# Start-up loads of a fused convolution, Fourier and feed-forward kernel: Fourier matrices issued after the other weights, small loads issued by ScalarE

## The chip, the cores and the metric

The kernel runs on one core of a Trainium2 chip. The time is the device time of one launch in microseconds (us); lower is better. One core has a matrix engine (TensorE, PE in the profile), three engines for elementwise work (VectorE or DVE, ScalarE or ACT, GpSimd or POOL) and SyncE (SP), which in this kernel issues nearly all DMA transfers. Each engine executes its own instruction stream in order; engines wait for each other and for transfers through semaphores.

## The reference, cut to what matters

The input x holds 32 images of 56 x 56 pixels and 96 channels. Two layers follow each other:

```python
# layer 0: mixture-of-experts convolution, one image b at a time
rw  = sigmoid(mean(x, axis=(1, 2)) @ Wr + br)                 # 4 expert weights per image
h   = relu(bn1(x @ sum_e(rw_e * Wpw_e) + rw @ bpw))           # 96 -> 384 channels
h   = relu(bn2(sum_e(rw_e * depthwise3x3(h, Wdw_e) + ...)))
x   = bn3(h @ sum_e(rw_e * Wpwl_e) + rw @ bpwl) + x           # 384 -> 96 channels
# layer 1, on the 3136 pixels of an image as tokens
t   = x + attn(layernorm(x))   # 96 -> 192, relu, FFT over 3136 tokens, relu(X * d + b), inverse FFT, 192 -> 96
out = t + ffn(layernorm(t))    # 96 -> 384 -> 96, inputs and weights rounded to 8-bit floats
```

The expert weights rw depend on the image, so the kernel mixes the four experts' weights anew for each image before it can multiply with them. The FFT over 3136 = 56 x 56 tokens is computed as products with four constant matrices, called `dfta`, `dftb`, `dftc` and `dftd`.

## The kernel before

The kernel has two parts. The first is a prologue (lines 326 to 526 or so), which loads all weights into on-chip memory and folds the batch-norm scales into them. It is scheduled automatically: the framework orders its instructions on each engine from their dependencies. The second part is a loop over the 32 images that is ordered by hand: a planner (`Plan`, lines 131 to 235) simulates the engines with fixed costs, takes steps of twelve streams (loads, mixing, expansion, convolution on TensorE, convolution on VectorE, projection, forward transform and so on), and emits their instructions in the order that it finds. Whatever the prologue does, the planner's order is the same.

Steps of the first image, in the order in which they depend on each other:

- `mixing` (line 572): VectorE sums the image (`pooled`, one TENSOR_REDUCE) and spreads the mean over 128 columns (`pool_b`); TensorE multiplies it with `wr_s` (`ps_rw`); VectorE adds the bias (`rw`), ScalarE applies the sigmoid. VectorE then mixes the expansion weights (`wk`, from `wpw_s`), all small vectors such as biases and 3x3 taps (`prod`, a product with `stk_s`, and `small`, its sum over the experts), and the projection weights (`wk2`, from `wpwl_s`). SyncE copies rotated parts of `wk2` to other partitions.
- `expansion` (line 642): TensorE multiplies the image with `wk` (`ps_pw`); ScalarE moves each result to `hp` with its bias from `small`. Four PSUM buffers exist for all steps together.
- `convolved_tensor` (line 677): the depthwise convolution as products with small diagonal matrices (`ps_dw<-hp,diag`), where GpSimd builds `diag` from `small`. `convolved_vector` (line 721) does a part of it on VectorE (`h<-hp,small,h`).
- `projection` (line 747, `ps_pwl`), then `forward` (line 813), whose product `ps_a<-ha,dfta_s` is the first use of `dfta`. `dftc` and `dftd` are used later still.

`psum()` (line 317) also issues up to 40 filler products `dftb_s` x `dftb_s` ahead of a step where the planner expects TensorE to be idle (`matmul(ps[:PB, 0:PB], dftb_s, dftb_s)`, line 321 in the profile).

Loads of the prologue: all are issued by SyncE, in the order in which they stand in the text: `wr_s`, image 0, `row_s`, `wpw_s`, `vec_s`, `stk_s`, `wpwl_s`, `w1c`, `dfta_s`, `dftb_s`, then twelve small loads into `w2_s` and `nl_s` (lines 367 and 368; `nl_s` is gathered in single 4-byte elements), `dftc_s`, `dftd_s`. Once VectorE has scaled `stk_s`, SyncE copies parts of it to other partitions of `stk_s`, six copies in all (line 494). Last come `f1` and `f2`, the feed-forward weights, and images 1 and 2.

The framework gives each SyncE or ScalarE transfer one of eight completion semaphores in turn. A transfer is only issued when the previous transfer on the same semaphore has landed.

On-chip memory is given out by pools. `prep` (line 335) holds what only the prologue needs (`row_s`, `f1`, `f2` and so on) and is closed at line 512. The pools `mix` (line 515) and `strip` are opened after that and take its place in memory. So the first tiles of `mix`, which belong to the mixing of image 0, wait for the last uses of what lay in `prep`.

Of the kernel before, what the change touches and what calls it, by code (L numbers as in the profile page):

```python
# [40 lines left out]
F32 = mybir.dt.float32  # L41
# [7 lines left out]
C = 96  # L49
M = 384  # L50
NC3 = M // 128
S = 56
N = S * S
CH = 192
K1 = S // 2 + 1
NQ = S // 2
PA = 4 * K1
KR = 2 * K1
PB = 2 * S
# [226 lines left out]
def kernel(  # L286
# [19 lines left out]
    nc = tc.nc  # L306
# [7 lines left out]
    def const(shape, dt, name):  # L314
        return cp.tile(shape, dt, tag=name, name=name)
# [16 lines left out]
    wr_s = const([C, NE], F32, "wr_s")  # L332
    nc.sync.dma_start(wr_s, wr)
    nc.sync.dma_start(xs[0], x[0])
    prep = tc.tile_pool(name="prep", bufs=1)
    pp = prep.__enter__()
    row_s = pp.tile([128, NROWS], F32, tag="row_s", name="row_s")
# [9 lines left out]
    nc.sync.dma_start(wpwl_s, wpwl)  # L347
    w1c = const([C, CH], F32, "w1c")
    nc.sync.dma_start(w1c, w1t)
    dfta_s = const([PB, NQ, PA], F32, "dfta_s")  # L350
    nc.sync.dma_start(dfta_s, dfta)
    dftb_s = const([PB, PB], F32, "dftb_s")
    nc.sync.dma_start(dftb_s, dftb)

    w2_s = const([128, NKIND, 2, C], F32, "w2_s")
    nc.gpsimd.memset(w2_s, 0.0)
    nl_s = const([128, 4, NKIND], F32, "nl_s")
    lo = VECS["rd"][0]
    in_vecs = vecs[:, lo : lo + 8].rearrange("p (n h) -> p n h", h=2)
    for kind in range(NKIND):  # L360
        at = 128 * kind
        while at < 128 * kind + 128:

            ch, p = at % CH, at - 128 * kind
            h, c = divmod(ch, C)
            n = min(C - c, 128 - p)
            nc.sync.dma_start(w2_s[p : p + n, kind, at // CH, :], w2t[c : c + n, h, :])
            nc.sync.dma_start(nl_s[p : p + n, :, kind], in_vecs[c : c + n, :, h])
            at += n
    dftc_s = const([PB, PB], F32, "dftc_s")  # L370
    nc.sync.dma_start(dftc_s, dftc)
    dftd_s = const([PA, NQ, PB], F32, "dftd_s")
    nc.sync.dma_start(dftd_s, dftd)

    ident = const([128, 128], F32, "ident")
    make_identity(nc, ident)

# [119 lines left out]
            )  # L497


    f1 = pp.tile([C, M], F32, tag="f1", name="f1")  # L500
    nc.sync.dma_start(f1, fw1t)
    nc.vector.tensor_copy(fw1, f1, saturate=False)
    f2 = pp.tile([128, NC3, C], F32, tag="f2", name="f2")
    nc.sync.dma_start(f2, fw2t)
    nc.vector.tensor_copy(fw2, f2, saturate=False)
    q1 = pp.tile([128, NC3], E5M2, tag="q1", name="q1")
    nc.vector.tensor_copy(q1, vec("fb1"), saturate=False)
# [4 lines left out]
    prep.__exit__(None, None, None)  # L512


    mixp = ctx.enter_context(tc.tile_pool(name="mix", bufs=2))
    sp = ctx.enter_context(tc.tile_pool(name="strip", bufs=1))


# [683 lines left out]
```

## Time and profile before

Times and busy shares are those of the profiled execution, except for the first row.

| | |
|---|---|
| median of 3 runs | 4453.47 us (4447.76 to 4464.15) |
| profiled execution, device time | 4452.19 us |
| profiled execution, span from first to last instruction | 4450.0 us |
| TensorE products, busy | 4284.4 us, 96% |
| TensorE weight loads, busy | 3152.2 us, 71% |
| VectorE busy | 3512.3 us, 79% |
| ScalarE busy | 2626.6 us, 59% |
| GpSimd busy | 978.8 us, 22% |
| TensorE busy, 0 to 50 us | 9.61 us |
| TensorE busy, 50 to 100 us | 46.16 us |
| TensorE busy, 100 to 200 us | 99.69 us |
| mean granted TensorE clock | 0.994 |

The page gives a span of 4450.0 us and 114,927 instructions. TensorE is busy nearly everywhere except in the first 50 us, which are the prologue. The view of stretches of time shows it: TensorE is idle from 0 to 27 us and again from 36.7 to 53.8 us, and what it does between them is mostly the filler products.

### The profile page before, as it was taken

The numbers are of one execution on the slowest core, as the hardware profiler recorded it, in microseconds if no ns is written. First come the engines' busy times: TensorE is split into PE (matmuls) and PEld (weight loads), VectorE is DVE, ScalarE is ACT, GpSimd is POOL, SyncE is SP. The second block draws the span as 40 slices with busy tenths as digits, with TensorE's granted clock in tenths as the row PEclk, the third lists the DMA queues.
The fourth block names the chain that finished last, engine by engine and source line by source line (L and its number), as shares of the span: only waits on it lengthen the run. The fifth ranks groups of instructions, "written<-read, shape, count | busy, mean of one in ns | idle before, by whom it ended". The sixth has DMA issues, their size and how long they took to land.

```text
span 4450.0 us, 114927 instructions
## 1 busy us (share of the span) xinstructions
PE 4284.4 (96%) x48916; PEld 3152.2 (71%) x48916; DVE 3512.3 (79%) x7222; ACT 2626.6 (59%) x4135; POOL 978.8 (22%) x1012
## 2 busy tenths in 40 slices
PE   6999999999999999999999999999999999999998
PEld 4767677677777677777677777677777777776778
DVE  6768787788877888778888778888788888778863
ACT  2455666655656565656565666556566656566654
POOL 1011222122222122222222222212222212222222
PEclk9999999999999999999999999999999999999999
DMA  3222332222332322332322332322332322332221
GB/s 91 55 65 64 81 91 78 72 75 71 81 83 71 87 71 75 81 83 71 87 69 73 85 83 71 87 70 67 90 80 72 82 65 76 93 80 71 76 77 49
DMA packets 305448, 339.19 MB, mean 76 GB/s; under 512 B 127908, under 2 KB 244452, under 8 KB 301636
## 3 DMA queue, kind: packets, MB, share of 16 engines
q1 hardware_dynamic: 304936, 331.85, 28.2%
q8 instruction: 384, 6.29, 0.6%
q14 instruction: 128, 1.05, 0.1%
HBM read 164.06 MB, written 158.27 MB: 72 GB/s over the span
## 4 chain that ended last, share of the span: by engine, by line
PE 67%; DVE 13%; ACT 8%; DMA 7%; issue 4%; POOL 1%; SPq 1%; POOLq 0%; ACTq 0%; DVEq 0%
PE ps_dw L553 14%; PE ps_pwl L553 11%; PE ps_w L553 11%; PE ps_pw L553 8%; PE ps_a L553 5%; DVE h L282 5%; PE ps_b L553 4%; PE ps_f L553 4%; DMA x<-in_x_dram 4%; PE ps_c L553 2%; DMA yd<-zo 2%; ACT z L282 2%; DVE z L282 2%; ACT mir L282 2%; PE ps_t_f L557 2%
## 5 line engine op out<-in xcount | busy, mean ns | idle before, releaser
L282 DVE SCALAR_TENSOR_TENSOR h<-hp,small,h 128x1792 f32<-128x1792 f32 (+2 forms) x768 | 1292.9, 1683 | 47.6 <-ACT h L282 31.8
L553 PE MATMUL ps_dw<-hp,diag 32*32 32x448 f32 x27648 | 858.7, 543 | 14.7 <-issue 14.6
L553 PEld LDWEIGHTS ps_dw<-hp,diag 32*32 32x32 f32 x27648 | 537.2, 103 | 281.7 <-issue 96.6
L282 POOL CAST h<-h 128x784 fp8e5<-128x784 f16 x384 | 382.6, 1022 | 1181.6 <-DVE h L282 1181.6
L553 PE MATMUL ps_pw<-x,wk 96*128 96x448 f32 (+1 forms) x1344 | 571.2, 564 | 34.5 <-DVE z L282 33.9
L553 PE MATMUL ps_pwl<-h,wk 128*96 128x448 f32 x1344 | 526.3, 539 | 0.0
L282 ACT ACTIVATE hp<-ps_pw,small 128x896 f32<-128x896 f32 (+2 forms) x384 | 361.3, 953 | 268.0 <-PE ps_pw L553 267.7
L282 ACT ACTIVATE nt<-yt,nm,rstd_f 112x96 fp8e5<-112x96 f32 x896 | 334.5, 454 | 201.0 <-DVE nm L282 200.8
L553 PEld LDWEIGHTS ps_pw<-x,wk 96*128 96x128 f32 x1344 | 244.6, 190 | 259.5 <-issue 186.5
L282 POOL TENSOR_TENSOR x<-x,y 96x784 f32<-96x784 f32 x128 | 286.8, 2241 | 551.2 <-DVE y L282 528.2
L553 PEld LDWEIGHTS ps_w<-w_s,z 128*112 128x112 f32 (+1 forms) x2816 | 361.5, 181 | 56.0 <-issue 48.4
L553 PE MATMUL ps_w<-w_s,z 128*112 128x96 f32 (+2 forms) x2816 | 376.7, 288 | 9.8 <-issue 9.2
L282 ACT ACTIVATE h<-ps_dw,small 128x448 f32<-128x448 f32 x384 | 214.9, 630 | 288.0 <-PE ps_dw L553 288.0
L553 PEld LDWEIGHTS ps_pwl<-h,wk 128*96 128x96 f32 x1344 | 209.5, 163 | 239.5 <-issue 228.5
L282 DVE SCALAR_TENSOR_TENSOR ha<-ps_w,rstd_a,nshift 112x192 f32<-112x192 f32 x896 | 308.2, 408 | 86.6 <-PE ps_w L553 86.6
L553 PEld LDWEIGHTS ps_b<-dftb_s,g 112*128 112x128 f32 x2816 | 334.8, 192 | 15.9 <-issue 13.2
L553 PE MATMUL ps_w<-w1c,x 96*112 96x192 f32 x1792 | 329.6, 329 | 9.9 <-ACT h L282 7.1
L553 PE MATMUL ps_b<-dftb_s,g 112*128 112x112 f32 x2816 | 339.0, 274 | 0.0
L553 PE MATMUL ps_a<-ha,dfta_s 112*116 112x192 f32 x1792 | 329.6, 330 | 7.7 <-ACT hp L282 7.4
L553 PEld LDWEIGHTS ps_a<-ha,dfta_s 112*116 112x116 f32 x1792 | 286.0, 181 | 36.5 <-ACT hp L282 31.0
L553 PEld LDWEIGHTS ps_w<-w1c,x 96*112 96x112 f32 x1792 | 284.6, 177 | 37.2 <-ACT h L282 18.9
L282 ACT ACTIVATE z<-ps_b,nl_s 128x448 f32<-128x448 f32 (+2 forms) x384 | 248.7, 689 | 88.3 <-PE ps_b L553 88.0
(160 smaller groups left out, 6197.7 us busy)
## 6 DMA issues: line engine op xcount, KB each, us to landing
gd<-g SPq DMA_DIRECT2D x128, 336.0 KB
g<-gd SPq DMA_DIRECT2D x32, 1344.0 KB
x<-in_x_dram SPq DMA_DIRECT2D x32, 1176.0 KB
yt<-yd SPq DMA_DIRECT2D x128, 294.0 KB
out_dram<-x SPq DMA_DIRECT2D x128, 294.0 KB
g<-gd SPq DMA_DIRECT2D x32, 1092.0 KB
gd<-g SPq DMA_DIRECT2D x128, 252.0 KB
yd<-zo SPq DMA_DIRECT2D x96, 336.0 KB
```

What stands on the lines that cost most here:

```text
L282: return getattr(self.namespace, name)(out, *args, **kw)
L553: nc.tensor.matmul(to, lhsT, rhs, start=start, stop=stop)
L557: nc.tensor.transpose(to, ap, eye)
```

## The change

Four things change in the prologue; none of the computation changes.

1. The pool `mix` is opened before `prep`, so it no longer shares memory with it.
2. `f1` and `f2` are loaded right after `dftb_s`. `dfta_s`, `dftc_s` and `dftd_s` are loaded after the code that issues the six copies of `stk_s`.
3. The twelve small loads into `w2_s` and `nl_s` are issued by ScalarE.
4. The streams of the planner and their order are left as they are.

```diff
     nc.sync.dma_start(wr_s, wr)
     nc.sync.dma_start(xs[0], x[0])
+    mixp = ctx.enter_context(tc.tile_pool(name="mix", bufs=2))
     prep = tc.tile_pool(name="prep", bufs=1)
...
     nc.sync.dma_start(w1c, w1t)
-    dfta_s = const([PB, NQ, PA], F32, "dfta_s")
-    nc.sync.dma_start(dfta_s, dfta)
     dftb_s = const([PB, PB], F32, "dftb_s")
     nc.sync.dma_start(dftb_s, dftb)
+    f1 = pp.tile([C, M], F32, tag="f1", name="f1")
+    nc.sync.dma_start(f1, fw1t)
+    f2 = pp.tile([128, NC3, C], F32, tag="f2", name="f2")
+    nc.sync.dma_start(f2, fw2t)
...
-            nc.sync.dma_start(w2_s[p : p + n, kind, at // CH, :], w2t[c : c + n, h, :])
-            nc.sync.dma_start(nl_s[p : p + n, :, kind], in_vecs[c : c + n, :, h])
+            nc.scalar.dma_start(w2_s[p : p + n, kind, at // CH, :], w2t[c : c + n, h, :])
+            nc.scalar.dma_start(nl_s[p : p + n, :, kind], in_vecs[c : c + n, :, h])
             at += n
-    dftc_s = const([PB, PB], F32, "dftc_s")
-    nc.sync.dma_start(dftc_s, dftc)
-    dftd_s = const([PA, NQ, PB], F32, "dftd_s")
-    nc.sync.dma_start(dftd_s, dftd)
-
     ident = const([128, 128], F32, "ident")
...
-    f1 = pp.tile([C, M], F32, tag="f1", name="f1")
-    nc.sync.dma_start(f1, fw1t)
+    dfta_s = const([PB, NQ, PA], F32, "dfta_s")
+    nc.sync.dma_start(dfta_s, dfta)
+    dftc_s = const([PB, PB], F32, "dftc_s")
+    nc.sync.dma_start(dftc_s, dftc)
+    dftd_s = const([PA, NQ, PB], F32, "dftd_s")
+    nc.sync.dma_start(dftd_s, dftd)
+
+
     nc.vector.tensor_copy(fw1, f1, saturate=False)
-    f2 = pp.tile([128, NC3, C], F32, tag="f2", name="f2")
-    nc.sync.dma_start(f2, fw2t)
     nc.vector.tensor_copy(fw2, f2, saturate=False)
...
     prep.__exit__(None, None, None)
...
-    mixp = ctx.enter_context(tc.tile_pool(name="mix", bufs=2))
     sp = ctx.enter_context(tc.tile_pool(name="strip", bufs=1))
```

Since the prologue is ordered by the framework, the text alone does not give the order of instructions. As built, the changed program differs from the one before as follows:

- SyncE issues `wr_s`, image 0, `row_s`, `wpw_s`, `vec_s`, `stk_s`, `wpwl_s`, `w1c`, `dftb_s`, `f1`, `f2`, `dfta_s`, `dftc_s`, `dftd_s`, image 1, then the six copies of `stk_s`, image 2 and the copies of `wk2`. Image 1 thus stands ahead of the copies of `stk_s`; before, it stood behind them.
- ScalarE issues the twelve small loads as its first instructions, ahead of its first activation. The last six of them each wait for an earlier transfer on the same semaphore, the tenth for the landing of image 0.
- Because the eight semaphores are now shared between the two issuers, each SyncE load from `row_s` to `dftb_s`, and `f2`, waits for one of the small loads to land (`row_s` for the fourth small load, `w1c` for the tenth, `f2` for the twelfth); `f1` waits for `row_s`, `dfta_s` for `wpw_s`, `dftc_s` for `vec_s`, `dftd_s` for `stk_s`, image 1 for `wpwl_s`, the copies of `stk_s` for `w1c`, `dftb_s`, `f1`, `f2`, `dfta_s` and `dftc_s` in this order, and image 2 for `dftd_s`.
- On VectorE, `pooled` and `pool_b` of image 0 stand at places 2 and 14 of its stream, where before they stood at places 79 and 80, behind the whole prologue. `nrd<-nl_s`, which waits for all six loads of `nl_s`, stands at place 12 instead of 75. `fw1` and `fw2`, the casts of `f1` and `f2`, stand ahead of `rw`.
- On GpSimd, TensorE and in all later parts of every stream the order of instructions is the same. The waits of the first `mix` tiles for the prologue (on `ps_rw`, on the GpSimd memset of `rw`, on ScalarE's table load ahead of the sigmoid, on the first copy of `wk2`) are gone.

## Prediction

> **What bounds the kernel now.** I read the page first: PE is busy 96% of the span, and of its 40 slices only the first is low. So the steady loop belongs to TensorE, and its order, which the change leaves alone, would have to change for it to get faster. What the change can reach is the prologue. There I read the chain of waits over the first 150 us:
>
> ```profile
> 14.98 10.40 DMA dfta_s<-in_dfta_dram
> ...
> 29.16 18.08 DMA dftd_s<-in_dftd_dram
> 47.23 0.02 issue
> 47.25 2.17 DMA f<-in_fw2t_dram
> 49.42 0.02 issue
> 49.45 0.32 DVE fw L505
> ...
> 53.84 0.56 PE ps_rw L553 x2
> 54.40 7.01 PE ps_pw L321 x54
> 61.41 8.09 PE ps_pw L553 x20
> 69.50 8.73 PE ps_dw L553 x281
> ```
>
> The columns are start, length and what. The reader is to see that two Fourier matrices, 10.40 and 18.08 us, stand on the chain, that `f2` comes behind `dftd`, that VectorE's cast of `f2` ends the prologue at 49.8, and that only then image 0 is summed and the first real product runs at 53.84. From 61.41 TensorE does not stop again.
>
> The waits of the first 70 us name the same place:
>
> ```profile
> DVE fw L502 <- DMA f<-in_fw1t_dram: 17.3, 1, 17.3
> DVE w_s L442 <- DMA w_s<-in_w2t_dram: 3.2, 1, 3.2
> ```
>
> The 17.3 us are the gap. `f1` was issued at 34.27 (timeline of SyncE), behind `dftd` at 29.16, and has only 144 KB, yet it landed at 48.5, after `dftd`. So small transfers issued behind `dftd` queue behind it. The view by stretches says why `dftd` is slow:
>
> ```profile
> 4.00:6.00 2.00, 0.00 (x0) 0.00 (x0) 2.00 (x3) 0.00 (x0) 2.00 (x3) 1.00 0.99 238
> ...
> 40.00:44.00 4.00, 0.00 (x0) 0.00 (x0) 0.00 (x0) 0.00 (x0) 0.00 (x0) 0.58 0.25 103
> 44.00:46.00 2.00, 0.00 (x0) 0.00 (x0) 0.00 (x0) 0.00 (x0) 0.00 (x0) 0.50 0.24 98
> ```
>
> The last columns are granted clock, mean share of the 16 DMA engines and GB/s: image 0 uses all 16 at 238 GB/s, `dftd` a quarter of them at about 100. And the timeline of VectorE behind the gap, start and length first:
>
> ```profile
> 58.56 0.35 DVE L282 TENSOR_TENSOR prod<-stk_s,rw 128x200 f32<-128x200 f32 x1
> 58.95 0.36 DVE L282 TENSOR_REDUCE small<-prod 128x40 f32<-128x200 f32 x1
> ...
> 61.74 3.41 DVE L282 TENSOR_REDUCE pooled<-x 96x1 f32<-96x3136 f32 x1
> ...
> 67.58 10.57 DVE L282 SCALAR_TENSOR_TENSOR h<-hp,small,h 128x1792 f32<-128x1792 f32 x5 [2.11 <-ACT h L282]
> ```
>
> **What the Trainium skill says.** "DMA: Bandwidth & Descriptors", section "Why a DMA increments its semaphore by 16 and not by 1": a transfer is spread over the largest number of engines up to 16 that divides its slowest dimension. `dftd` has 116 rows, so 4; the trace agrees (share 0.25). `dfta` and every image, with 112 and 96 rows, get 16. The same page, "Queues, rings and completion order": SyncE and ScalarE each have one ring on the same 16 engines, served in ring order within a ring and in turn between rings; the late `f1` agrees with the first half, the second no trace here shows. The same page, "Issuing engines are not separate DMA queues": issuing from a second engine saves only issue time. "TensorE: Matmul & The Clock Gate", "What's actually happening": half clock after an idle window of about 3.4 us; here TensorE stops at 36.7 and the clock reads 0.58 in 40 to 44.
>
> **The change part by part.**
>
> *Pool moved.* `pooled` no longer waits for the prologue; it runs when image 0 lands, 7 to 9 us (before, `row_s`, the next in the queue with 962 KB, was there at 11.3, and takes 4 us of that at 220 to 240 GB/s; the small loads now run beside it). Its 3.4 us lie where VectorE only waits for `row_s`. On VectorE, 3.4 + 0.3 us leave the path after 49.8. ScalarE's table load (1.28 us, at 54.74 behind `rw`) can now run early.
>
> *Small loads on ScalarE.* VectorE's 3.2 us wait for `w2_s` goes. ScalarE has nothing to do until `row_s` is there. New: SyncE's loads wait for small loads. `row_s` now waits for a small load instead of being issued at 1.64. A small transfer took 2.17 us from issue to landing (`f2`, on idle engines), so it is issued near 5 to 7 and its bytes follow image 0's almost without a gap; from below 0, from above 8 x 2.17 = 17 us if all eight hand-offs come one after another. Most run in parallel, because ScalarE issues six without a wait; I take 2 us. `nrd` at place 12 of VectorE waits for the last small load (issued once image 0 is there, so about 12 to 13); behind it wait the batch-norm steps, which wait for `row_s` until about 13 anyway.
>
> *TensorE.* `ps_shift` started at 27.99; less 3.2 for the lost wait, plus 2 for `row_s`, plus about 0.7 for `pool_b`, `nrd` and three multiplications of `w2_s` that come earlier: 27.5. First fillers 7.9 us (28.80 to 36.71 before), `ps_rw` 0.6, second fillers 7.2, so `ps_pw` could start near 43.5 and ScalarE evacuate 1.95 us later (63.20 less 61.25): 45.5.
>
> *The Fourier matrices and the copies of `stk_s`.* This sets the end. `prod` needs all six copies of `stk_s`. They are issued when VectorE is done with `stk_s` (about 31 us), but behind `dftd` and now also behind image 1 on the same ring. A quarter of their rows lie on the four engines of `dftd`. Before, `dfta` landed at 25.38. Now `dftb`, `f1` and `f2` (49 + 144 + 144 KB, 1.5 us at 230 GB/s) go ahead of it and the hand-offs cost 2: 29. `dftd`: 1421 KB at about 100 GB/s, less what of its 18.08 us is start-up since its bytes follow at once: 16.5, so 45.5. Image 1's quarter of 1176 KB on those engines at 100 GB/s: 3, so 48.5; the copies and landing 1. Copies here at 49.6. They were not late before, because `prod` stood at 58.56 behind everything else.
>
> *Sum.* `prod` and `small` take 0.75 us (58.56 to 59.31), so `small` is there at 50.4 and ScalarE evacuates at once, where before it did at 63.20: 12.8 us earlier. From there to the first `ps_dw` (69.43) ScalarE's work is the same 6.2 us. VectorE must first do `wk2` (2.5) and `pooled` of image 1 (3.7), so its `h` starts at 56.6 instead of 67.58, 11.0 earlier; it was not what held TensorE then (`h` ended at 87.60, `ps_pwl` came at 94.15), so only some of the difference of 1.8 counts. I take 12 us. TensorE's second stop, from 52 to 56.4, is broken by one `ps_pw` group, so I charge nothing for the clock; if it does fall to half, it costs up to 3.4, one window. `dfta` is first used at 117.73, image 2 and the `wk2` copies later than they land: free. The loop keeps order and waits; 12 us carry to the end since TensorE is on the chain throughout.
>
> The profiled execution took 4452.19 us: 4440.2. The median of the runs is 1.3 above it: 4441.5, which I round to 4441.
>
> **The rivals.**
>
> A, the sum above: 4441, with the landing of the copies from 47 to 53 and the clock: 4437 to 4447.
>
> B, the copies pass `dftd`, or image 1 is not ahead of them on those engines: then the filler chain decides, evacuation at 45.5, 17.7 us earlier than 63.20: 4436. For it: 144 KB of `f1` is no 1 KB copy. Against it: `f1` waited on the whole of `dftd`.
>
> C, the change does not do what it says: the matrices are not last, image 1, the copies of `stk_s` and of `wk2` stand behind them, so if the copies land near 60 the prologue ends as late as it did: 4453. Against it: that needs 10 us more than the sum of bytes.
>
> D, slower: the eight hand-offs between SyncE and ScalarE come one after another, 17 us instead of 2. The copies then land at 64.6 and `ps_dw` starts 7 us later, at 71.6, 2 us later than 69.43; and TensorE, idle for more than 10 us, starts at half clock, 3.4 more: 4459. It decides from the point where the copies land after 62.4. For it: 1536 single elements in `nl_s`, and waits for image 0 in the middle of the chain. Against it: ScalarE issues half of the loads without any wait.
>
> E, over 22 us gained: only if the loop itself, moved in memory and in time against the clock windows, runs better. Nothing in the profile asks for it.
>
> **How the numbers follow.** A 0.70, B 0.12, C 0.08, D 0.06, E 0.04. About 0.5% (22 us) is what a measurement of this kernel tells from no change; the three runs before differ by 16. Below 4431: E, and part of B by scatter: 0.08. Slower than 4476: a part of D with more stalls behind it, 0.04. Within: 0.88. The range takes A with 5 us of scatter, B, and the near side of C: 4430 to 4454.
>
> **What would show it right or wrong.** `pooled` of image 0 near 9 us; `ps_rw` near 36; SyncE's issue of image 1 ahead of the copies; VectorE waiting in front of `prod` for a DMA into `stk_s`, with `prod` near 50; `ps_dw` first near 56; from there on the same lengths. `prod` near 37 says B; `row_s` later than 16 and `dfta` later than 33 say C or D. A difference that grows after 150 us would make the whole approach wrong.

## The result and the profile after

The median fell from 4454.16 us (8 runs, 4447.76 to 4464.15) to 4435.16 us (8 runs, 4431.78 to 4445.83): ratio 0.9959, 95% interval 0.9945 to 0.9974, 19 us. On a second chip it was 11 us: 4446.85 (51 runs) to 4435.84 (10 runs), 0.9974 (0.9964 to 0.9985). The profiled execution after has a span of 4429.7 us where before's had 4450.0.

To see where the 20.3 us lie, I cut each profile at the sum of image 2 (`pooled<-x` in the timeline of VectorE), the first point at which the loop runs as it does for every later image. In before it starts at 148.44, after at 140.33. So the start gave 8.1 us and the loop, 4301.5 to 4289.3, gave 12.2. The loop's share was forecast as nothing; it has a part of its own below.

The start first. The chain of waits of after over the first 150 us (start, length, what) has the stations that took the place of `dfta`, `dftd` and `f2`:

```profile
1.20 7.77 DMA nl_s<-in_vecs_dram
10.30 7.50 DMA nl_s<-in_vecs_dram
...
31.36 0.83 PE ps_shift L455 x4
...
36.68 16.45 DMA stk_s<-stk_s
...
54.09 2.01 ACT hp L282 x2
```

Two small loads that ScalarE now issues lead, and the last copy of `stk_s` takes 16.45 us. The waits of the first 70 us in after (total, times, longest) say the same from VectorE's side:

```profile
DVE prod L282 <- DMA stk_s<-stk_s: 10.6, 1, 10.6
...
DVE nrd L488 <- DMA nl_s<-in_vecs_dram: 2.6, 1, 2.6
DVE s1row L415 <- DMA row_s<-in_rows_dram: 1.8, 1, 1.8
```

The 17.3 us for `f1` have gone; 10.6 us for the copies came in, and shorter waits for `nl_s` and `row_s` ahead of them. SyncE's timeline in after shows what stands ahead of the copies:

```profile
9.34 0.35 SPq L339 DMA_DIRECT2D row_s<-in_rows_dram  x1
...
20.94 0.38 SPq L503 DMA_DIRECT2D dftd_s<-in_dftd_dram  x1
22.01 0.32 SPq L282 DMA_DIRECT2D x<-in_x_dram  x1
33.48 3.78 SPq L492 DMA_DIRECT2D stk_s<-stk_s  x6
```

`row_s` goes out at 9.34 instead of 1.64. The queue's own waits in after name what held it, a small load with the same semaphore:

```profile
SPq L339 <- DMA w_s<-in_w2t_dram: 7.7, 1, 7.7
```

The Fourier matrices are the last of the weights, yet image 1 and the copies still stand behind them, image 1 first. By the semaphore updates in the trace `dftd` landed at 48.06, image 1 at 51.40 and the copies from 51.66 to 53.13. The stretches of after (busy time of TensorE, its weight loads, VectorE, ScalarE and GpSimd, then granted clock, mean share of the DMA engines, GB/s) show both ends of that queue:

```profile
42.00:44.00 2.00, 2.00 (x23) 2.00 (x22) 0.61 (x1) 0.00 (x0) 0.00 (x0) 1.00 0.25 100
46.00:48.00 2.00, 2.00 (x7) 0.98 (x6) 0.00 (x0) 0.00 (x0) 0.00 (x0) 1.00 0.25 101
50.00:52.00 2.00, 1.60 (x5) 0.51 (x3) 0.00 (x0) 0.00 (x0) 0.00 (x0) 1.00 1.03 264
54.00:56.00 2.00, 0.75 (x1) 0.50 (x2) 1.89 (x4) 1.91 (x2) 1.65 (x3) 0.50 0.11 31
...
62.00:64.00 2.00, 2.00 (x58) 1.42 (x36) 1.97 (x2) 0.00 (x0) 0.00 (x0) 0.58 0.03 8
```

Until 48 a quarter of the engines carries `dftd`; from then on image 2, issued at 48.08, fills the others while image 1's rest and the copies follow on that quarter. TensorE runs out of work at 51.6 and finds half clock when it comes back. Its timeline in after:

```profile
39.51 0.30 PE L554 MATMUL ps_rw<-wr_s,pool_b 96*128 96x4 f32 x2
39.66 5.54 PE L321 MATMUL ps_pw<-dftb_s 112*112 112x112 f32 x54
45.04 6.57 PE L554 MATMUL ps_pw<-x,wk 96*128 96x504 f32 x16
55.25 3.73 PE L554 MATMUL ps_pw<-x,wk 96*128 96x504 f32 x4 [3.64 <-ACT hp L282]
59.22 10.91 PE L554 MATMUL ps_dw<-hp,diag 32*32 32x448 f32 x288 [0.24 <-POOL rw L282]
```

The first `ps_dw` starts 10.2 us earlier than before (69.43) but takes 10.91 us instead of 8.80, because its first 4.4 us run at half clock, which the clock record shows from 53.43 to 63.67. 10.2 less 2.1 is the 8.1.

### The profile page after: what moved, and what is told of

Its sections match the earlier page's. It is cut to its first block, busy times and chain, and to the rows that moved or that the text cites. A ratio compares the mean times of both kernels' runs of the same rounds, so it can differ in the third digit from the quotient of the medians.

```text
span 4429.7 us, 114914 instructions
## 1 busy us (share of the span) xinstructions
PE 4278.0 (97%) x48916; PEld 3145.0 (71%) x48916; DVE 3503.1 (79%) x7222; ACT 2626.4 (59%) x4135; POOL 979.1 (22%) x1012
## 3 DMA queue, kind: packets, MB, share of 16 engines
q8 instruction: 384, 6.29, 0.6%
## 4 chain that ended last, share of the span: by engine, by line
PE 66%; DVE 15%; ACT 8%; DMA 7%; issue 3%; POOL 1%; SPq 0%; ACTq 0%; POOLq 0%; DVEq 0%
PE ps_dw L554 14%; PE ps_pwl L554 11%; PE ps_w L554 10%; PE ps_pw L554 7%; DVE h L282 6%; PE ps_a L554 5%; PE ps_b L554 4%; PE ps_f L554 4%; DMA x<-in_x_dram 4%; PE ps_c L554 2%; ACT z L282 2%; DMA yd<-zo 2%; DVE z L282 2%; ACT mir L282 2%; DVE pooled L282 2%
## 5 line engine op out<-in xcount | busy, mean ns | idle before, releaser
L282 DVE SCALAR_TENSOR_TENSOR h<-hp,small,h 128x1792 f32<-128x1792 f32 (+2 forms) x768 | 1292.6, 1683 | 33.0 <-ACT h L282 17.3
```

The costliest lines, as they stand in the source:

```text
L282: return getattr(self.namespace, name)(out, *args, **kw)
```

## The experiments

Each row is one kernel's profile; "loop" is the span less the start of image 2's sum, "half clock" the time at half clock after 150 us in the trace's clock record, which runs 2.3 to 2.7 us past the last instruction; "ratio" compares the medians of all runs with those of before on the same chip.

| kernel | `prod` | sum of image 2 | loop | half clock | ratio to before |
|---|---|---|---|---|---|
| before | 58.56 | 148.44 | 4301.5 | 42.8 | 1 |
| before_again | 56.37 | 146.97 | 4297.3 | 41.1 | 0.9998 (0.9987 to 1.0009) |
| before_third | 57.32 | 147.17 | 4304.7 | 46.1 | single run |
| before_fourth | 60.55 | 151.68 | 4303.8 | 47.2 | single run |
| after | 53.21 | 140.33 | 4289.3 | 26.6 | 0.9959 (0.9945 to 0.9974) |
| after_again | 52.52 | 139.79 | 4293.4 | 30.5 | 0.9974 (0.9964 to 0.9985) |
| nofill (= after) | 52.09 | 138.51 | 4292.0 | 26.8 | single run |
| pool_only | 48.63 | 137.61 | 4290.2 | 32.7 | 0.9977 (0.9969 to 0.9984) |
| no_pool | 52.47 | 140.21 | 4293.5 | 29.9 | 0.9975 (0.9968 to 0.9982) |
| split_d | 43.79 | 133.45 | 4295.2 | 36.9 | 0.9961 (0.9946 to 0.9976) |
| small_on_sp | 49.39 | 135.72 | 4287.8 | 22.7 | 0.9960 (0.9943 to 0.9976) |
| pool_split | 40.80 | 130.45 | 4295.1 | 37.1 | 0.9950 (0.9934 to 0.9966) |
| split_nofill | 38.75 | 128.34 | 4292.2 | 37.2 | 0.9951 (0.9932 to 0.9969) |
| best_start | 39.08 | 127.03 | 4295.5 | 33.3 | 0.9938 (0.9925 to 0.9952) |

**Both kernels once more.** They ask whether the loop's 12 us belong to the change. Theory W: the loop's difference is half clock that falls at chance. Theory P: the `mix` tiles lie elsewhere in memory and the loop is faster for it.

> The kernel before once more, for a second profile. In the first profile the image loop, from the sum of image 2 (148.4 us) to the end (4450.0), took 4301.6 us; in the changed kernel's it took 4289.4 (140.3 to 4429.7). Theory W (clock windows): that loop difference of 12 us comes from how many stretches of half clock fall into an execution, with no difference between the programs; then this profile's loop can be anywhere from 4285 to 4305 and follows the number of half-clock stretches. Theory P (placement): the loop is slower because of where the mix tiles lie in memory; then 4300 to 4303 again. Both: sum of image 2 at 148.4 within 0.5.

> The changed kernel once more. Theory W: loop anywhere from 4285 to 4305, following the number of half-clock stretches. Theory P: 4288 to 4291 again. Both: sum of image 2 at 140.3 within 0.5, copies of stk_s landing at 53.

Before's loop came out at 4297.3 and after's at 4293.4, 3.9 us apart. P's ranges were missed in both, by 2.7 and 2.4 us; W, which allowed 4285 to 4305, was met, but so wide a range tests little. Before's start missed too: image 2's sum at 146.97, where 148.4 was expected from another chip.

**The pool move alone**, the rest as before:

```diff
     nc.sync.dma_start(xs[0], x[0])
+    mixp = ctx.enter_context(tc.tile_pool(name="mix", bufs=2))
     prep = tc.tile_pool(name="prep", bufs=1)
...
-    mixp = ctx.enter_context(tc.tile_pool(name="mix", bufs=2))
```

> Only the mix pool moved, loads as before. Theory of the copies (what ends the prologue is dftd on four DMA engines, with the copies of stk_s and f1 behind it): small of image 0 comes right after f1 lands near 48.5, so first evacuation near 49, first ps_dw near 55, sum of image 2 near 138 to 139, which is 10 us earlier than before and as good as the whole change or better. Rival (the order of the loads makes the gain): sum of image 2 stays above 145. Loop: P says 4288 to 4291, W says unrelated to the program.

Image 2's sum at 137.61, where 138 to 139 was expected: this one line gives 10.8 us of the start against before's first profile (9.4 against before_again on the same chip), more than the whole change. VectorE waits again for the copies, in the waits of pool_only:

```profile
DVE prod L282 <- DMA stk_s<-stk_s: 10.0, 1, 10.0
```

But a second wait decides here. The first `ps_dw` starts 14.6 us earlier than in before (54.79 for 69.43), more than the sum of image 2 gains. VectorE's `h` starts only 8.4 us earlier, at 59.17, since VectorE first waits for image 1, in its timeline of pool_only:

```profile
55.52 3.42 DVE L282 TENSOR_REDUCE pooled<-x 96x1 f32<-96x3136 f32 x1 [3.03 <-DMA x<-in_x_dram]
```

Image 2's sum comes 78.44 us after this `h`, and just as long after it in split_nofill and best_start below, which also wait for image 1.

**The change without the pool move**, `mix` opened where before had it:

> The whole change without the move of the mix pool. Theory of the copies: image 0 is summed only near 35 us, but prod waits for the copies of stk_s until 53 anyway, so sum of image 2 at 140 to 141, as with the whole change: here the pool move is not what gains. Rival (the pool move gains): sum of image 2 near 148. Loop: P says 4300 to 4303, as before, W says unrelated to the program.

140.21, as expected, and the same as with it (138.5 to 140.3 in three profiles). Its waits show another VectorE instruction in front, `nrd`, which in this order stands second:

```profile
DVE nrd L487 <- DMA nl_s<-in_vecs_dram: 17.3, 1, 17.3
...
DVE prod L282 <- DMA stk_s<-stk_s: 7.3, 1, 7.3
```

The copies absorb even that. So each half of the change ends at the same queue behind `dftd`, and the two do not add. And P falls: with the `mix` tiles where before has them the loop took 4293.5, not 4300.

**`dftd` in two pieces**, of 112 and 4 rows, so that its bulk can use 16 DMA engines instead of 4:

```diff
-    nc.sync.dma_start(dftd_s, dftd)
+    nc.sync.dma_start(dftd_s[0:112], dftd[0:112])
+    nc.sync.dma_start(dftd_s[112:PA], dftd[112:PA])
```

> The whole change, with dftd loaded as 112 rows and 4 rows, which also lets the framework put image 1 behind the copies of stk_s. Theory of the copies (dftd on four DMA engines holds back the quarter of the copies that lies on them): dftd done near 36 instead of 48, copies landed by 41, prod right behind wk near 43 instead of 52.5, then the filler products are last: first evacuation near 46.7, first ps_dw near 52 without a half clock in it, sum of image 2 at 131 to 133 against 139.8. Rival (the copies are late because a queue of this many bytes is, whatever engines they lie on): prod not before 49, sum of image 2 at 137 or later.

The stretches of split_d have the queue empty by 34, where after's was busy with `dftd` up to 48:

```profile
30.00:32.00 2.00, 1.40 (x4) 0.89 (x4) 2.00 (x11) 0.00 (x0) 0.00 (x0) 1.00 1.05 295
32.00:34.00 2.00, 2.00 (x12) 1.98 (x12) 1.85 (x19) 0.00 (x0) 0.00 (x0) 1.00 0.49 117
34.00:36.00 2.00, 2.00 (x13) 2.00 (x13) 0.69 (x7) 0.00 (x0) 0.00 (x0) 1.00 0.07 15
```

`prod` no longer waits for a DMA, and TensorE has no second stop. Its timeline in split_d:

```profile
40.89 5.54 PE L321 MATMUL ps_pw<-dftb_s 112*112 112x112 f32 x54
46.27 8.26 PE L555 MATMUL ps_pw<-x,wk 96*128 96x504 f32 x20
54.45 8.80 PE L555 MATMUL ps_dw<-hp,diag 32*32 32x448 f32 x288
```

Image 2's sum came at 133.45, 6.1 us ahead of the mean of the three afters (139.5), in place of 131 to 133: the filler products ahead of `ps_rw` took 8.59 us instead of 7.57. They are the next limit. The split is not the only thing that differs here: as the expectation says, image 1 now stands behind the copies. pool_split below shows the split alone.

**Small loads back on SyncE**, the rest as in the change:

```diff
-            nc.scalar.dma_start(w2_s[p : p + n, kind, at // CH, :], w2t[c : c + n, h, :])
-            nc.scalar.dma_start(nl_s[p : p + n, :, kind], in_vecs[c : c + n, :, h])
+            nc.sync.dma_start(w2_s[p : p + n, kind, at // CH, :], w2t[c : c + n, h, :])
+            nc.sync.dma_start(nl_s[p : p + n, :, kind], in_vecs[c : c + n, :, h])
```

> The whole change with the twelve small loads issued by SyncE again, behind f2 and ahead of dfta. Theory of the hand-offs (loads that share semaphores between the two issuers wait for each other, and row_s came 3 us late for it): row_s lands at 11.5 instead of 14.4, the copies land near 48 instead of 52.5, since image 1 is behind them here, first ps_dw near 54, sum of image 2 at 135 to 138 against 139.8: the part of the change done by ScalarE costs some 3 us. Rival (ScalarE's issue gains, for it takes twelve issues off SyncE): sum of image 2 later than 140.

135.72, as expected: 3.8 us better than the mean of the afters. `row_s` goes out at once, in SyncE's timeline of small_on_sp:

```profile
1.65 0.43 SPq L339 DMA_DIRECT2D row_s<-in_rows_dram  x1
```

The expectation put the gain on `row_s`, and its numbers came, but the record gives another cause. TensorE did get to `ps_shift` earlier (27.05 for 31.29), yet `prod` still waited 10.0 us for the copies, and `dftd`, behind which they queue, landed at 48.14, no earlier than in after (48.06). What moved is image 1. In this order it stands behind the copies, in the same timeline:

```profile
29.25 3.76 SPq L492 DMA_DIRECT2D stk_s<-stk_s  x6
33.06 15.41 SPq L282 DMA_DIRECT2D x<-in_x_dram  x2
```

The last row holds images 1 and 2; the first of them is issued at 33.06. So the copies landed at 48.32 to 49.27, right after `dftd`, where in after image 1 came between. Issuing the small loads from ScalarE is a loss in this kernel, but through image 1's place in the order that the framework made of it, and not through `row_s`. Image 1 alone was not moved.

**The pool move and the split together**, everything else as before:

> Only the mix pool moved and dftd split into 112 and 4 rows, loads otherwise as before. Theory of the copies: copies land near 37.5, then the fillers are last: first evacuation near 43.5, first ps_dw near 49, sum of image 2 at 130 to 132, 16 us earlier than before and 6 earlier than with the pool move alone. Rival: no earlier than 136.

130.45, as expected, 18 us ahead of before with two small edits. Image 1 stands behind the copies here and in pool_only, so the pair shows the split alone: 137.61 to 130.45, 7.2 us. The first `ps_dw`, expected near 49, came at 51.46.

**The split without image 0's fillers.** Left out are the filler products of `psum()` for image 0's `ps_rw` and first `ps_pw`, whose results nothing reads.

```diff
-        if plan is not None:
+        if plan is not None and name not in ("ps_rw_0", "ps_pw_0_0_2_0"):
```

> The whole change with dftd split, and without the 54 filler products ahead of the first ps_rw and the first ps_pw (they compute nothing that is used). Theory (with the copies in time, the fillers are what ends the prologue): prod near 41, first evacuation near 42, first ps_dw near 47, sum of image 2 at 127 to 130, at most 4 us of it lost to a half clock. Rival (the fillers pay for themselves by keeping the clock up): sum of image 2 at 132 or later.

128.34, as expected: 5.1 us for the fillers. `ps_pw` starts 9.0 us earlier than in split_d, but now falls into half clock, in TensorE's timeline of split_nofill:

```profile
32.33 0.59 PE L555 MATMUL ps_rw<-wr_s,pool_b 96*128 96x4 f32 x2
37.27 11.61 PE L555 MATMUL ps_pw<-x,wk 96*128 96x504 f32 x20 [4.35 <-DVE wk L282]
```

11.61 us instead of 8.26: the fillers kept the clock up, and 3.35 us of the 9.0 are paid back. VectorE then waited 4.21 us for image 1, the next thing in the queue.

**nofill.** This label was to take the fillers out of the change with `dftd` in one piece. By a slip the edit was missing, and what ran is the changed kernel itself; the expectation stays untested, and the run serves as a third profile of after.

> The changed kernel without the filler products in front of image 0's ps_rw and first ps_pw (nothing reads their results); dftd stays in one piece. Theory of the copies: they land at 53 whatever TensorE does, so prod stays at 52.5 to 53.5 and the sum of image 2 at 139 to 141, although ps_pw starts near 37 instead of 45. Rival (the 54 fillers are a limit of their own beside the copies): the sum of image 2 at 131 to 134, as with the split.

**All three gains of the start together**, split_nofill with the small loads on SyncE:

> The changed kernel with dftd loaded in two pieces, of 112 and of 4 rows, with the small loads back on SyncE, and without image 0's filler products: the three gains of the start together. The start then gives what the earlier run with the split and without fillers gave (sum of image 2 at 128.3), less the 4 us that ScalarE's issue cost: 123 to 126, with image 1's landing as the next thing waited for. If row_s is not what leads the start any more, it stays at 127 to 129. Whole run, by theory W (half-clock stretches vary from run to run and owe nothing to the program): the start is 22 to 25 us shorter than before's 148.4, so the median is 4422 to 4428 beside a before of 4446 to 4449; a median under 4415 would say that the loop too runs better in this kernel.

The median fell from 4453.41 to 4423.22, ratio 0.9938: the best version of this study. It lies inside the 4422 to 4428 expected, but beside a before of 4453.41 and not of 4446 to 4449: 30.2 us were gained, of which the start gives some 21.5. The start missed its first range, 123 to 126, and came at 127.03, in the second, where `row_s` no longer leads. `ps_pw` did start 4.4 us earlier than in split_nofill (32.90 for 37.27), its first part at half clock in both (11.68 and 11.61 us). But `prod` waited 6.23 us for the copies, and came at 39.08 for 38.75, and image 1 landed only 1.3 us earlier (44.91 for 46.22). VectorE waited 2.57 us for it, and `h` and image 2's sum came 1.3 us earlier, no more. This agrees with the reading of small_on_sp.

**Before twice more, for its loop.** By then two profiles of before had longer loops than all ten others. Theory L: something in before's start makes its loop longer.

> The kernel before once more, for its loop. So far two profiles of before spent 4301 and 4297 us from the sum of image 2 to the end, with 43 and 41 us of half clock after 150 us; ten profiles of kernels with another start and the same loop spent 4288 to 4296, with 23 to 37 us of half clock. Theory W (half clock falls at chance, whatever the start): with two more profiles of before, at least one lies at or under 4294, with under 37 us of half clock. Theory L (something of before's start makes its loop longer): both lie at 4297 or above, with 40 us or more.

> As for the third profile of before: theory W has at least one of the two at or under 4294 us from the sum of image 2 to the end, theory L has both at 4297 or above.

4304.7 and 4303.8, with 46 and 47 us of half clock: by these limits W falls and L holds. Both profiles are from one further chip, on which no other kernel ran; that its loops are longer whatever the kernel is not ruled out.

## What is known of the loop's 10 us

The four profiles of before have loops of 4297.3 to 4304.7 (mean 4301.8), the ten others 4287.8 to 4295.5 (mean 4292.4). pool_only and no_pool have no edit in common, and both have the short loop. So it is not one edit's work on the loop; it looks like a loss of before's own, which each of the other starts removed. That is a comparison of profiles, and not yet a cause.

The medians of many runs say that 10 us is the upper end. On the second chip (51 runs of before) after, pool_only and no_pool are 11.0, 10.9 and 10.5 us faster, of which their starts, against before_again's, give 7.2, 9.4 and 6.8: 1.5 to 3.8 us are left for the loop. The same estimate, with the mean start of before, gives 3.6 to 5.4 for the four kernels of the third chip, 8.7 for best_start and 10 for the first pair.

One piece of it can be pinned. The time from image 4's sum to image 5's is 136.0 to 138.9 us in the four profiles of before and 133.3 to 134.3 in the ten others: 3.75 us between the means, with no overlap. At that place the timeline of before reads (all engines; the brackets give idle time and its releaser):

```profile
521.98 0.56 ACT L282 COPY zo<-ps_w 112x480 f32<-112x480 f32 x1 [4.49 <-DMA yd<-zo]
...
522.59 1.97 PE L553 MATMUL ps_c<-zo,dftc_s 112*112 112x384 f32 x4 [2.02 <-ACT zo L282]
```

and that of after:

```profile
512.71 0.56 ACT L282 COPY zo<-ps_w 112x480 f32<-112x480 f32 x1 [2.89 <-DMA yd<-zo]
...
513.32 1.08 PE L554 MATMUL ps_c<-zo,dftc_s 112*112 112x384 f32 x4 [0.42 <-ACT zo L282]
```

ScalarE may fill `zo` again only when its last contents have been stored. That store ended 1.6 us later in before, TensorE stood still for 2.02 us instead of 0.42, and the stretches of before show what followed:

```profile
518.00:520.00 2.00, 2.00 (x18) 1.81 (x17) 1.93 (x4) 0.00 (x0) 0.00 (x0) 1.00 0.69 176
520.00:522.00 2.00, 0.56 (x6) 0.39 (x4) 1.70 (x3) 0.02 (x1) 0.00 (x0) 0.97 0.03 4
522.00:524.00 2.00, 1.41 (x2) 0.76 (x3) 0.00 (x0) 0.53 (x1) 0.00 (x0) 0.50 0.00 0
```

Half clock lasts from 521.89 to 528.72, by the clock record. All four profiles of before have half clock here, and none of the ten others. ScalarE's wait at this store is 4.15 to 4.54 us in all four profiles of before and 2.71 to 3.00 in the others.

The store's own records say what made it late. The page lists a queue with which the chip loads instructions (`q8 instruction: 384, 6.29, 0.6%` in both kernels, 16,384 bytes a packet). One such packet starts 8.0 to 8.4 us after the start of image 4's sum in all four profiles of before and takes 0.9 to 1.0 us; the last elements of the store leave behind it, and the store ends at 9.2 to 9.8. In the profile shown here, 21 of the store's 912 packets were left, and the first of them starts at 9.11, when the packet is through. In the ten others the same store ends at 8.2 to 8.3. The packet's time does not tell the groups apart: in eight of the ten it starts at 7.8 to 8.3 too, in split_d with 119 of the store's packets still to start, and the store is untouched. The trace does not say on which DMA engine a packet ran. So the packet explains how the store came late in before, and why it did no harm in the others stays open, as do the remaining some 6 us of the loop, which are spread over several images where the two groups overlap.

For the first pair the sum closes. Over their profiles (four and three) before and after differ by 9.0 us in the start (148.57 to 139.54) and by 10.2 in the loop (4301.8 to 4291.6): 19.2, where the first chip's medians differ by 19.0. On the second chip the pair of profiles gives 7.2 in the start and 3.9 in the loop, together the 11 of its medians. So the loop's part is half of the gain on the first chip and a third on the second.

## Why the prediction was right, and where it was not

The time was right to 6 us and inside the range, but not for the reasons given: two errors of opposite sign met, the start gained 3 to 4 us less than forecast and the loop, by the pairs of profiles, 4 to 12 more. That they nearly cancelled was luck.

- *Pool moved.* `pooled` of image 0 at 8.80, as said (near 9). pool_only shows the line's worth alone.
- *Hand-offs between ScalarE and SyncE: "I take 2 us".* Mis-sized. `row_s` is used 3.05 us later than before (14.36 to 11.31), and `nrd`, said to wait until 12 or 13 without cost, waited until 18.03, with VectorE's batch-norm steps behind it: `ps_shift` at 31.29 instead of 27.5, `ps_rw` at 39.51 instead of near 36. The 2.17 us from issue to landing came from `f2` on idle engines. The small loads did run in parallel, but the seven that were issued behind the first landed one after the other at 8.97 to 10.05, right behind image 0 (8.78); the one that `row_s` waits for took 7.1 us. The Trainium skill ("DMA: Bandwidth & Descriptors", "Issuing engines are not separate DMA queues") promises only issue time from a second engine; here the shared semaphores held `row_s` back for 7.7 us in return. None of this set the end, though: `dfta`, with the 2 us in its sum, landed at 28.93, for 29.
- *Copies behind `dftd` and image 1.* The mechanism was right, named as what sets the end: `prod` waited for them. Expected 49.6, measured 53.21, and the 3.6 us lie behind `dfta`: `dftd` landed at 48.06 for 45.5, image 1 took 3.3 us more for 3, the copies 1.7 for 1. `dftd` was given about 100 GB/s throughout. While image 1 ran on the other engines (28 to 32 us), a packet of 12,544 bytes, one row of either, took 0.97 us in the median; with `dftd` alone (34 to 48) it took 0.47. The quarter of the engines is confirmed: four completions of `dftd` are in the trace, and in split_d, with 112 rows in one piece, the loads have all but passed by 34, where `dftd` alone lasted to 48, which agrees with the Trainium skill (same page, "Why a DMA increments its semaphore by 16 and not by 1"). Rival B, copies that pass `dftd`, is out.
- *Evacuation, `ps_dw`, `h`.* Late by what the copies were late: 54.09 for 50.4, 59.22 for 56.4, 60.05 for 56.6.
- *"I charge nothing for the clock".* Wrong: TensorE stood from 51.6 to 55.25 and the first `ps_dw` cost 2.1 us more. The 3.4 named as the worst case was not exceeded. split_d, without that stop, has 8.80.
- *Sum of the start.* 12 us forecast; 8.1 in this pair, 9.0 over all profiles.
- *"12 us carry to the end"; "The loop keeps order and waits".* This is the step that failed. The order is kept; the waits are not. The loop became shorter, by 12.2 us in this pair and 3.9 on the second chip, and the prediction's own test, a difference that grows after 150 us, came out against it. Rival E had the place ("moved in time") but not the mechanism, and its "Nothing in the profile asks for it" was half true: before's profile shows the 4.49 us in front of `zo` and the half clock behind, which the prediction passed over.

## What to carry to other kernels

A transfer whose row count leaves it on few DMA engines holds back everything behind it on its ring, so it is better split into a piece that spreads and a rest (7.2 us here) than moved to the end of a queue that has no end. When an edit changes the order of a queue, look at what else changed place in it before the gain is put on the edit. Two edits that each lead to the same next wait do not add: try each alone before both are kept. And when a start is shifted, cut the profile where the loop begins and count both parts over several profiles; agreement of the total can hide two errors.

## What had not been expected of the hardware

- A store and an instruction load can meet: in four of four profiles of before, one packet of 16,384 bytes held the end of a store back by 1.0 to 1.6 us, TensorE stood still for 1.69 to 2.07 us instead of 0.24 to 0.54, and half clock followed: 3.75 us between two images. In eight other profiles a packet at the same place did nothing.
- Half clock comes in stretches of 3.41 us or twice that (the last one, which runs past the end, apart), 5 to 11 of them behind 150 us, and several fall at the same places in many of the profiles. A stop of 1.69 us was enough for it in before_again, half of the 3.4 us of idle time that the prediction reckons with.
- Small loads took 5.2 to 7.8 us beside large ones on another queue and landed right behind them. With the DMA engines nearly idle, loads of the same shapes took 1.6 to 2.5 us (in before, those issued from 25.40 on).
- Filler products that nobody reads kept 3.35 us of clock, while they delayed `ps_pw` by 9.0 us.
